# Layer 1's softmax sums over keys: from matmuls with ones to turned blocks on VectorE

## The chip, the core and the metric

The kernel runs on one core of a Trainium2 chip. The metric is the device time of one execution in microseconds (us). A core has five engines with their own instruction streams: TensorE (PE in the profile; its weight loads are PEld), VectorE (DVE), ScalarE (ACT), GpSimd (POOL) and SyncE (SP), which here issues nearly all DMA transfers. They meet through semaphores.

## What is computed

Two gated transformer-like blocks on x of 4 x 1024 x 512, in float32. The change is in the attention of the second block (layer 1):

```python
x = x + s * g                      # layer 0
xn = _layernorm(x, axis=-1)
# _L1_attn_ref(xn, wq, wk, wv, wo), 16 heads of 32
q, k, v = (proj(wq), proj(wk), proj(wv))
sin, cos = rope_tables(t, HD, dtype=x.dtype)
q, k = apply_rope(q, k, sin, cos)
att = jnp.einsum('bhqd,bhkd->bhqk', q, k) * (1.0 / math.sqrt(HD))
att = jax.nn.softmax(att, axis=-1)
y = jnp.einsum('bhqk,bhkd->bhqd', att, v)
y = y.transpose(0, 2, 1, 3).reshape(b, t, c)
return y @ wo.T
# then g = silu(_L1_ffn_ref(xn, ...)), and x + s * g is returned
```

The softmax needs, for every query and head, the maximum over 1024 keys, the exponentials, and their sum over keys, by which the weighted values are divided.

## The kernel before, in words

Layer 0 comes first, then layer 1's attention, then layer 1's feed-forward part. Only the attention concerns us. It works in 32 *units* (`units`, `nu` = 32): batch b (4), group g of four heads (4), half qh of the queries (512 each). Unit u has 8 key blocks kb of 128 keys (`TB` = 8). The loop over `s` goes through *slots*, eight per unit, and a slot holds work of several units at once:

- `top(u, j, pair, mx)`, two calls a slot, with u, j = divmod(s, 8): PE multiplies 128 queries with 512 keys for two heads into a tile `sq`, and VectorE takes the maximum over keys into `mx`. I call the two maxima of a slot a and b. At j = 7 the maxima of the unit are folded; `turn_max` one slot later transposes them on VectorE (`mt`) and sends them through DRAM (`turned_d`) into `mT`.
- `exps(e)` with e = s - 12 (`LAG` = 12): `expo` has PE multiply the keys of block kb with 512 queries of four heads into two tiles `sk`, adding the negative maxima by a matmul with `onesr` and `mT`; ScalarE takes the exponentials into `pT` (keys on partitions, 4 heads x 512 queries in the free axis; three buffers). Then the key blocks of a unit are added up into one tile `part`, by GpSimd (by VectorE in the last 12 slots). So unit u's key block 0 has its turn in slot 4 of unit u+1, and key block 7 in slot 3 of unit u+2.
- `weigh` one slot later: PE multiplies `pT` with the values into `y`. ScalarE copies `y` to `yr` after the last block.
- `total` and `divide` in slot 6 of unit u+2 (before the change): PE sums `part` over the 128 partitions, that is over keys, by a matmul with a tile of ones, four heads at once; the result `z` has the sum repeated over each head's 32 partitions. ScalarE copies it to `zs`, VectorE takes the reciprocal in four pieces, GpSimd multiplies `yr` with it into `yT`. Unit 30 (`nu - 2`) has no `part`: PE sums its eight `pT` directly. Unit 31 does so for its first four and adds up the others on VectorE.
- In between, `advance` puts quarters of other chains on PE: the projections of the next group of heads (`heads_in`: `wk`, `wq`, `v`), and the output projections `wo_out`, listed in `soon` for a later slot. For `wk` and `wq` each half is rotated: ScalarE copies it to `raw`, eight DMAs on SP put its halves into `rr`, VectorE multiplies (`wkT`, `wqT` with `cs`), and GpSimd does two operations (`rr` times `cs`, then the addition), called the `rr` pair here.

PSUM tiles of `sq` and `sk` come from one pool tag, `ring`, with three buffers in rotation, in the order sq a, sq b, sk, sk; projections use `acc1` with one buffer.

PE's order is that of the source (`manual_schedule` for PE). The instructions of the other engines are put in order by the framework's scheduler, by dependencies and its own estimate of when each can run; each engine then runs its instructions in the compiled order. `keep_in_program_order` pins single instructions.

Of the kernel before, what the change touches and what calls it, by code (L numbers as in the profile page):

```python
# [12 lines left out]
F32 = mybir.dt.float32  # L13
# [3 lines left out]
ALU = mybir.AluOpType  # L17
AX = mybir.AxisListType

P = 128  # L20
B, N, D = 4, 1024, 512
NT = B * N
H, HD = 16, 32
# [12 lines left out]
def kernel(ctx, tc, ins, out):  # L36
    nc = tc.nc
# [3 lines left out]
    dram = ctx.enter_context(tc.tile_pool(name="dram", bufs=1, space=bass.MemoryType.DRAM))  # L41
# [47 lines left out]
    def shared_tile(tag, name):  # L89
        return w0.tile([P, KD, D], F32, tag=tag, name=name)  # L90
# [155 lines left out]
    with ExitStack() as es:  # L246
# [4 lines left out]
        p2 = es.enter_context(tc.tile_pool(name="a0", bufs=2, reuse_waits="tile"))  # L251
# [318 lines left out]
    with ExitStack() as es:  # L570
# [3 lines left out]
        p2 = es.enter_context(tc.tile_pool(name="f0", bufs=2, reuse_waits="tile"))  # L574
# [126 lines left out]
        for g in range(NH0 * NBLK + 2 + 2 * TPB):  # L701
            blk, c = divmod(g, NH0)
            if g == NH0 * NBLK:

                for n in ("wk", "wq", "wv"):
# [3 lines left out]
                            out=W[n], in_=ins[n + "T"].rearrange("(k p) n -> p k n", p=P)  # L709
# [8 lines left out]
            for i in range(TPB):  # L718
                q = g - 2 - 2 * i
# [95 lines left out]
    with ExitStack() as es:  # L815
        wp = es.enter_context(tc.tile_pool(name="a1c", bufs=1, reuse_waits="tile"))
        p2 = es.enter_context(tc.tile_pool(name="a1", bufs=2, reuse_waits="tile"))

        def ring(name):
            return pp.tile([P, 2, 512], F32, tag="ring", name=name, bufs=3)  # L820

        def acc1(name):
            return pp.tile([P, 512], F32, tag="acc1", name=name)

        TB = N // P
# [4 lines left out]
        def load1(b):  # L830
# [15 lines left out]
        turned_d = [  # L846
            dram.tile([8, 512], F32, tag=f"turned{i}", name=f"turned_d{i}") for i in range(2)
        ]

        partner = []  # L850
        for i in range(2):
# [92 lines left out]
        def total(z, part, kb, n):  # L944

            for h in range(4):
                nc.tensor.matmul(  # L947
                    z[h * HD : (h + 1) * HD, :], lhsT=ones[:, :HD], rhs=part[:, h, :],
                    start=(kb == 0), stop=(kb == n - 1),
                )  # L950

        def divide(u, yr, z):

            b, g, qh = u
            zs = p2.tile([P, 512], F32, tag="zs", name=f"zs_{b}_{g}_{qh}", bufs=1)
            nc.scalar.copy(zs, z)
            yT = p2.tile([P, 512], F32, tag=f"yT{qh}", name=f"yT_{b}_{g}_{qh}", bufs=5 + qh)
            for c in range(TPB):
                cols = slice(c * P, (c + 1) * P)
                nc.vector.reciprocal(zs[:, cols], zs[:, cols])  # L960
            nc.gpsimd.tensor_tensor(yT, yr, zs, ALU.mult)
            yTs[b][g, qh] = yT
# [100 lines left out]
        def exps(e):  # L1063
            if not 0 <= e < TB * nu:
                return
            u, kb = divmod(e, TB)
            pT = pTs[e] = p2.tile([P, 4, 512], F32, tag="pT", name=f"pT_{e}", bufs=3)
            expo(u, kb, pT)


            if u == nu - 2:
                return
            k0 = TB // 2 if u == nu - 1 else 0
            add = nc.vector if e + LAG >= TB * nu else nc.gpsimd
            if kb == k0 + 1:
                parts[u] = p2.tile([P, 4, 512], F32, tag="part", name=f"part_{u}")
                add.tensor_tensor(parts[u], pTs[e - 1], pT, ALU.add)  # L1077
            elif kb > k0:
                add.tensor_tensor(parts[u], parts[u], pT, ALU.add)  # L1079
# [5 lines left out]
        units = [(b, g, qh) for b in range(B) for g in range(4) for qh in range(2)]  # L1085
        nu, LAG = len(units), TB + 4
        yTs = {b: {} for b in range(B)}
# [18 lines left out]
            tc.tile_pool(name="psuma", bufs=1, space=PSUM, reuse_waits="tile")  # L1106
        )
        must, spare = deque(), deque()
        mx, mTs, pTs, ys, parts, lates, soon = {}, {}, {}, {}, {}, {}, {}
        for s in range(TB * nu + LAG + 1):  # L1110

            e = s - LAG
            if s % (2 * TB) == 0 and s < TB * nu:

                assert not must
                n = s // (2 * TB) + 1
                if n < 4 * B:  # L1120
                    b, g = divmod(n, 4)

                    two = (nc.sync, nc.gpsimd) if s == 0 else (nc.sync, nc.sync)
                    must.extend(
                        heads_in(
                            b, g, acc1, {(w, h): two for w in ("wk", "wq") for h in range(2)}
                        )
                    )
                    if g == 3 and b + 1 < B:
                        load1(b + 1)  # L1130
                left = 2
            if s in soon and s < TB * nu:
                spare.extend(wo_out(*soon.pop(s), acc1))
            if s % 2 == 0:

                chain = None
                if spare and left and s < TB * nu:
                    chain = spare.popleft()
                    left -= 1
                elif must:  # L1140
                    chain = must.popleft()
            if s == 2 * TB:
                W["wo"] = shared_tile("wo", "wo")
                tc.keep_in_program_order(
                    nc.sync.dma_start(
                        out=W["wo"], in_=ins["woT"].rearrange("(k p) n -> p k n", p=P)
                    )
                )
            if s % 4 == 0 and s // 4 < TPB:
                lates[s + 2] = s // 4, late(s // 4)  # L1150
            if s < TB * nu:
                u, j = divmod(s, TB)
                if j == 0:
                    mx[u] = p2.tile([P, TPB, 4, 2], F32, tag="mx", name=f"mx_{u}")
                for pair in range(2):
                    top(u, j, pair, mx[u])
                if j == TB - 1:
                    m2 = twice[u % 2][:, :, :8].rearrange("p q (h c) -> p q h c", c=2)

                    w = p2.tile([P, TPB, 4, 2], F32, tag="m1", name=f"m1_{u}")  # L1160
                    nc.vector.tensor_reduce(
                        w[:, :, :, 0], mx.pop(u), AX.X, ALU.max, negate=True
                    )
                    for out, sign in ((w[:, :, :, 1], -1.0), (m2[:, :, :, 0], 1.0)):
                        nc.scalar.activation(
                            out.bitcast(F32R), w[:, :, :, 0], AF.Copy, scale=sign
                        )
                    nc.vector.tensor_reduce(m2[:, :, :, 1], w, AX.X, ALU.add)
            late_exp = s >= TB * nu
            if late_exp:  # L1170
                exps(e)
            if 1 <= e <= TB * nu:
                u, kb = divmod(e - 1, TB)
                if kb == 0:
                    ys[u] = pp.tile([P, 512], F32, tag="y", name=f"y_{u}")
                weigh(u, kb, pTs[e - 1], ys[u])
# [350 lines left out]
```

## Time and profile before

| | us |
|---|---|
| median of 3 runs (lowest, highest) | 3089.14 (3086.78, 3090.99) |
| the profiled execution | 3092.08 |
| its span, first to last instruction | 3090.2 |
| granted TensorE clock, mean | 0.996 |
| attention of layer 1: first `sq` maximum, first feed-forward matmul (`gate`) | 1163, 2598 |
| ScalarE busy in the span | 1173.7 |
| DMA issues on SP for `rr` in the span | 480 |

How to read it: a group line gives the kernel's line, the engine, the operation, what it writes and reads with shapes, the count, then busy time in us, the mean of one in ns, and the idle time of the engine just before them with what ended most of it. A timeline line gives start and length in us, engine, line, operation, tiles, shapes, how many instructions were merged into it, and in brackets the idle time before it and its releaser. A wait is put down to the engine that came last. The line of the chain of waits for `z` (L947) reads 1.2% of the span.

### The profile page before, as it was taken

The numbers are of one execution on the slowest core, as the hardware profiler recorded it, in microseconds if no ns is written. First come the engines' busy times: TensorE is split into PE (matmuls) and PEld (weight loads), VectorE is DVE, ScalarE is ACT, GpSimd is POOL, SyncE is SP. The second block draws the span as 40 slices with busy tenths as digits, with TensorE's granted clock in tenths as the row PEclk, the third lists the DMA queues.
The fourth block names the chain that finished last, engine by engine and source line by source line (L and its number), as shares of the span: only waits on it lengthen the run. The fifth ranks groups of instructions, "written<-read, shape, count | busy, mean of one in ns | idle before, by whom it ended". The sixth has DMA issues, their size and how long they took to land.

```text
span 3090.2 us, 61139 instructions
## 1 busy us (share of the span) xinstructions
PE 3038.3 (98%) x25985; PEld 1730.5 (56%) x25985; DVE 1788.3 (58%) x2569; ACT 1173.7 (38%) x1708; POOL 1557.9 (50%) x742
## 2 busy tenths in 40 slices
PE   9999999999999998999999999999999999999998
PEld 5555555578788873333334444333434436888886
DVE  4444555467777776555555555555555544566655
ACT  3111111145556542444444444444444454333332
POOL 1221212234443444888888988888988940001001
PEclk9999999999999999999999999999999999999999
DMA  4222232323223231100001000100000014222111
GB/s 137 86 86 86 86 86 72 127 96 100 95 92 110 96 129 52 36 9 9 9 18 42 16 10 15 43 16 14 10 18 15 13 46 152 82 69 75 58 52 56
DMA packets 113787, 186.81 MB, mean 60 GB/s; under 512 B 19809, under 2 KB 33633, under 8 KB 113377
## 3 DMA queue, kind: packets, MB, share of 16 engines
q1 hardware_dynamic: 106096, 161.30, 17.3%
q0 software_dynamic: 7280, 21.39, 1.9%
q8 instruction: 205, 3.36, 0.5%
q14 instruction: 78, 0.63, 0.1%
q10 hardware_dynamic: 128, 0.13, 0.0%
HBM read 115.11 MB, written 59.26 MB: 56 GB/s over the span
## 4 chain that ended last, share of the span: by engine, by line
PE 57%; DVE 1%; ACT 1%; POOL 1%; issue 0%; SPq 0%; DMA 0%; ACTq 0%; POOLq 0%; DVEq 0%
PE sk L1037 9%; PE sq L1007 8%; PE y L1056 8%; PE gate L1260 5%; PE up L1260 5%; PE dn L1282 5%; PE wo L862 4%; PE v1ps L862 3%; PE wk L862 3%; PE wq L862 3%; PE sk L1043 2%; PE z L947 1%; ACT pT L1048 1%; DVE zs L960 1%; POOL part L1079 0%; DVE mx L1011 0%
## 5 line engine op out<-in xcount | busy, mean ns | idle before, releaser
L1011 DVE TENSOR_REDUCE mx<-sq 128x2 f32<-128x1024 f32 x512 | 604.2, 1218 | 434.8 <-PE sq L1007 434.0
L1079 POOL TENSOR_TENSOR part<-part,pT 128x2048 f32<-128x2048 f32 x180 | 817.8, 4543 | 17.3 <-ACT pT L1048 8.9
L1048 ACT ACTIVATE pT<-sk 128x1024 f32<-128x1024 f32 x512 | 495.6, 1020 | 557.3 <-PE sk L1043 520.1
L1007 PE MATMUL sq<-wkT,wqT 32*128 32x512 f32 x2048 | 321.0, 639 | 10.0 <-ACT pT L1048 7.0
L1037 PE MATMUL sk<-wqT,wkT 32*128 32x512 f32 x2048 | 322.8, 641 | 0.8 <-DVE mx L1011 0.5
L1056 PE MATMUL y<-pT,v 128*32 128x512 f32 x2048 | 275.5, 608 | 0.1
L1304 POOL TENSOR_TENSOR th<-th,x 128x512 f32<-128x512 f32 x31 | 40.1, 1293 | 458.0 <-DVE th L1303 379.0
L646 PE MATMUL pj<-wpj,hp 128*128 128x512 f32 x1024 | 262.0, 396 | 4.0 <-DVE hp L606 4.0
L593 PE MATMUL fc<-xp,wfc 128*128 128x512 f32 x1024 | 259.0, 395 | 3.6 <-ACT h L598 2.8
L614 POOL TENSOR_TENSOR sums<-sums,h 128x512 f32<-128x512 f32 x112 | 163.1, 1456 | 195.0 <-ACT h L598 189.7
L1043 PE MATMUL sk<-mT,onesr 2*128 2x512 f32 x1024 | 235.7, 788 | 0.0
L382 PE MATMUL qk<-xnT,wqkv 128*128 128x512 f32 x512 | 228.7, 600 | 0.7 <-ACT xnT L156 0.7
L646 PEld LDWEIGHTS pj<-wpj,hp 128*128 128x128 f32 x1024 | 191.2, 188 | 51.9 <-DVE hp L606 10.5
L593 PEld LDWEIGHTS fc<-xp,wfc 128*128 128x128 f32 x1024 | 189.4, 188 | 47.2 <-ACT h L598 6.0
L606 DVE TENSOR_TENSOR hp<-h,hp 128x512 fp32r<-128x512 f32 x128 | 128.2, 1001 | 85.2 <-ACT hp L603 85.2
L1260 PE MATMUL gate<-xp,wf 128*128 128x512 f32 x704 | 174.2, 390 | 0.0
L1260 PE MATMUL up<-xp,wf 128*128 128x512 f32 x704 | 173.9, 389 | 0.0
L1037 PEld LDWEIGHTS sk<-wqT,wkT 32*128 32x128 f32 x2048 | 96.2, 184 | 138.3 <-issue 117.2
L1282 PE MATMUL dn<-wf,hp 128*128 128x512 f32 x704 | 173.6, 390 | 0.0
L1077 POOL TENSOR_TENSOR part<-pT,pT 128x2048 f32<-128x2048 f32 x30 | 136.4, 4548 | 72.1 <-ACT pT L1048 72.0
L1007 PEld LDWEIGHTS sq<-wkT,wqT 32*128 32x128 f32 x2048 | 89.9, 184 | 122.7 <-issue 85.5
L382 PEld LDWEIGHTS qk<-xnT,wqkv 128*128 128x128 f32 x512 | 95.0, 191 | 111.8 <-issue 104.5
(230 smaller groups left out, 4359.3 us busy)
## 6 DMA issues: line engine op xcount, KB each, us to landing
s<-s SPq DMA_DIRECT2D x96, 256.0 KB
xp<-xp_d SPq DMA_DIRECT2D x16, 1024.0 KB
x<-x SPq DMA_DIRECT2D x36, 256.0 KB
x<-in_x SPq DMA_DIRECT2D x32, 256.0 KB
raw_fc<-in_w_fcT SPq DMA_DIRECT2D x32, 256.0 KB
xp_d<-hi POOLq DMA_DIRECT2D x32, 256.0 KB, 2.7
xp_d<-xnT POOLq DMA_DIRECT2D x32, 256.0 KB, 2.9
x0r<-in_x SPq DMA_DIRECT2D x32, 256.0 KB
```

What stands on the lines that cost most here:

```text
L382: nc.tensor.matmul(a, lhsT=wqkv[k][:, c0 : c0 + P], rhs=xnTs[blk][:, k, :], start=(k == 0), stop=(k == KD - 1),)
L593: nc.tensor.matmul(a, lhsT=wfc[k][:, c * P : (c + 1) * P], rhs=xp[n][:, k, :].bitcast(F32R), start=(k == 0 and n == 0), stop=(k == KD - 1 ...
L646: nc.tensor.matmul(ds[i], lhsT=hparts[blk, c][n][:, i * P : (i + 1) * P], rhs=wpj[c], start=(c == 0 and n == 0), stop=(c == NH0 - 1 and n ...
L862: nc.tensor.matmul(out[r0 : r0 + HD, :], lhsT=lhsT[:, r0 : r0 + HD], rhs=rhs, start=start, stop=stop,)
L1007: nc.tensor.matmul(sq[:, hh, :], lhsT=qT[r, q0 : q0 + P], rhs=kT[r, n * 512 : (n + 1) * 512], start=True, stop=True,)
L1011: nc.vector.tensor_reduce(mx[:, qt, 2 * pair : 2 * pair + 2, n], sq, AX.X, ALU.max)
L1037: nc.tensor.matmul(sks[h // 2][:, h % 2, :], lhsT=kT[r, kb * P : (kb + 1) * P], rhs=qT[r, qh * 512 : (qh + 1) * 512], start=True, stop=False,)
L1048: nc.scalar.activation(pT[:, 2 * pair : 2 * pair + 2, :], sks[pair], AF.Exp, scale=QKS)
L1056: nc.tensor.matmul(y[r, :], lhsT=v[:, kb, r], rhs=pT[:, h, :], start=(kb == 0), stop=(kb == TB - 1),)
L1079: add.tensor_tensor(parts[u], parts[u], pT, ALU.add)
L1260: nc.tensor.matmul(a, lhsT=ws[n, c][:, k, :], rhs=xp[m][:, k, :], start=(k == 0 and m == 0), stop=(k == KD - 1 and m == 1),)
L1282: nc.tensor.matmul(ds[i], lhsT=hparts[blk, c][n][:, i * P : (i + 1) * P], rhs=w, start=(c == 0 and n == 0), stop=(c == NH1 - 1 and n == 1),)
```

## The change

The matmuls `total` for units 0 to 30 go. In their place VectorE transposes the `part` tile in blocks of 32 x 32 (`sums_of`, eight chunks of 256 columns) and sums each turned block along its rows; `gather` turns the collected 64 columns back and sends them through DRAM (`groups_d`) so that the four groups of 32 partitions lie beside one another; `invert` adds the four, takes the reciprocal of 64 columns on 32 partitions, and sends it through DRAM (`inverse_d`), from where four DMAs spread a row each over 32 partitions into `zs`; `times` multiplies on GpSimd. Unit 30 now has a `part` too: GpSimd adds its blocks up to 3, VectorE the blocks 4 to 7. In the source a unit's sums stand in slots 6 to 11 counted from the start of unit u+2, `gather` in slot 12, `invert` in slot 14, `times` in slot 16. The output projections start two slots after `times`, and in the last 16 slots up to 8 of them may start. `divide` stays for unit 31.

```diff
+        def sums_of(u, part, c):
+            if c == 0:
+                groups[u] = p2.tile([P, 64], F32, tag="groups", name=f"groups_{u}", bufs=1)
+            t = p2.tile([P, 256], F32, tag="keys", name=f"keys_{u}_{c}", bufs=1)
+            nc.vector.transpose(t, part.rearrange("p h q -> p (h q)")[:, c * 256 : (c + 1) * 256])
+            nc.vector.tensor_reduce(
+                groups[u][:, 8 * c : 8 * c + 8], t.rearrange("p (c a) -> p c a", a=HD), AX.X, ALU.add
+            )
+
+        def gather(u):
+            back = p2.tile([P, 64], F32, tag="back", name=f"back_{u}", bufs=1)
+            nc.vector.transpose(back, groups.pop(u))
+            at = groups_d[u % 2]
+            nc.sync.dma_start(out=at, in_=back)
+            sides[u] = p2.tile([P, 256], F32, tag="keys", name=f"sides_{u}", bufs=1)
+            nc.sync.dma_start(
+                out=sides[u][:HD, :].rearrange("c (i x) -> c i x", i=4),
+                in_=at.rearrange("(i c) x -> c i x", i=4),
+            )
+
+        def invert(u):
+            b, g, qh = units[u]
+            inv = p2.tile([P, 64], F32, tag="inv", name=f"inv_{u}", bufs=1)
+            nc.vector.tensor_reduce(
+                inv[:HD, :], sides.pop(u)[:HD, :].rearrange("c (i x) -> c x i", i=4), AX.X, ALU.add
+            )
+            nc.vector.reciprocal(inv[:HD, :], inv[:HD, :])
+            at = inverse_d[u % 2]
+            nc.sync.dma_start(
+                out=at.rearrange("a c b -> c a b"),
+                in_=inv[:HD, :].rearrange("c (a b) -> c a b", a=2),
+            )
+            zss[u] = p2.tile([P, 512], F32, tag="zs", name=f"zs_{b}_{g}_{qh}", bufs=1)
+            for h in range(4):
+                row = at[h // 2, 16 * (h % 2) : 16 * (h % 2) + 16, :]
+                nc.sync.dma_start(
+                    out=zss[u][h * HD : (h + 1) * HD, :],
+                    in_=row.rearrange("c b -> (c b)").partition_broadcast(HD),
+                )
+
+        def times(u, yr):
+            b, g, qh = units[u]
+            yT = p2.tile([P, 512], F32, tag=f"yT{qh}", name=f"yT_{b}_{g}_{qh}", bufs=5 + qh)
+            nc.gpsimd.tensor_tensor(yT, yr, zss.pop(u), ALU.mult)
+            yTs[b][g, qh] = yT
...
@@ exps
-            if u == nu - 2:
-                return
...
@@ the loop over s
-                left = 2
+                left = 2 if n < 4 * B else TB
...
+            zu, at = divmod(s - 6, TB)
+            zu -= 2
+            for u, i in ((zu - 1, at + TB), (zu, at)):
+                if u == nu - 2:
+                    if i == 0:
+                        for c in range(8):
+                            sums_of(u, parts[u], c)
+                        parts.pop(u)
+                    elif i == 1:
+                        gather(u)
+                    elif i == 3:
+                        invert(u)
+                    elif i == 5:
+                        times(u, ys.pop(u))
+                        soon[s] = units[u][0], units[u][2], yTs[B - 1]
+                elif 0 <= u < nu - 2:
+                    if i < 6:
+                        for c in ((0, 1), (2,), (3,), (4, 5), (6,), (7,))[i]:
+                            sums_of(u, parts[u], c)
+                        if i == 5:
+                            parts.pop(u)
+                    elif i == 6:
+                        gather(u)
+                    elif i == 8:
+                        invert(u)
+                    elif i == 10:
+                        times(u, ys.pop(u))
+                        b, g, qh = units[u]
+                        if g == 3:
+                            soon[s + 2] = b, qh, yTs[b]
...
-                if u >= nu - 2:
+                if u == nu - 1 and kb < TB // 2:
                     if kb == 0:
                         z_last = acc1(f"z_{u}")
-                    if u < nu - 1 or kb < TB // 2:
-                        total(z_last, pTs[e - 1], kb, TB)
+                    total(z_last, pTs[e - 1], kb, TB)
...
-                    yr = p2.tile([P, 512], F32, tag="yr", name=f"yr_{u}", bufs=1)
+                    yr = p2.tile([P, 512], F32, tag="yr", name=f"yr_{u}")
...
-                    if u == nu - 2:
-                        divide(units[u], ys.pop(u), z_last)
-                        soon[s] = units[u][0], units[u][2], yTs[B - 1]
             held = 0
-            zu = (s - 6) // TB - 2
             if s % TB == 0 and 0 < s <= TB * nu:
                 turn_max(s // TB - 1)
-            if s % TB == 6 and 0 <= zu < nu - 2:
-                z = ring(f"z_{zu}")[:, 0, :] if zu == nu - 3 else acc1(f"z_{zu}")
-                total(z, parts.pop(zu), 0, 1)
-                divide(units[zu], ys.pop(zu), z)
-                b, g, qh = units[zu]
-                if g == 3:
-                    soon[s + 4] = b, qh, yTs[b]
-            elif s in lates:
+            if s in lates:
                 late_turn(*lates.pop(s))
```

More of the change, by code (lines that the diff above doesn't have):

```diff
@@ L848 @@
         ]
+        groups_d = [dram.tile([P, 64], F32, tag=f"groups{i}", name=f"groups_d{i}") for i in range(2)]
+        inverse_d = [
+            dram.tile([2, HD, HD], F32, tag=f"inverse{i}", name=f"inverse_d{i}") for i in range(2)
+        ]
         partner = []
@@ L952, in divide @@
+        def times(u, yr):
[3 more added lines that the diff above has]
+            yTs[b][g, qh] = yT
         def divide(u, yr, z):
             b, g, qh = u
-            zs = p2.tile([P, 512], F32, tag="zs", name=f"zs_{b}_{g}_{qh}", bufs=1)
+            zs = p2.tile([P, 512], F32, tag="mT", name=f"zs_{b}_{g}_{qh}")
             nc.scalar.copy(zs, z)
@@ L1108 @@
         must, spare = deque(), deque()
+        groups, sides, zss = {}, {}, {}
         mx, mTs, pTs, ys, parts, lates, soon = {}, {}, {}, {}, {}, {}, {}
```

## The prediction

> **What bounds the kernel now.** First the page's busy times, then the window of layer 1's attention (about 1163 to 2598 us), then one unit of it instruction by instruction.
>
> ```profile
> PE 3038.3 (98%) x25985; PEld 1730.5 (56%) x25985; DVE 1788.3 (58%) x2569; ACT 1173.7 (38%) x1708; POOL 1557.9 (50%) x742
> ...
> L1011 DVE TENSOR_REDUCE mx<-sq 128x2 f32<-128x1024 f32 x512 | 604.2, 1218 | 434.8 <-PE sq L1007 434.0
> L1079 POOL TENSOR_TENSOR part<-part,pT 128x2048 f32<-128x2048 f32 x180 | 817.8, 4543 | 17.3 <-ACT pT L1048 8.9
> ```
>
> PE is busy all the time. VectorE waits only for PE's next `sq`, and GpSimd, 4.54 us per key block, is the engine with least to spare in this stage: 1115 of the 1300 us between 1200 and 2500 (its row of the busy times there). A slot with a quarter of a projection in it takes 5.25 us (the `sq` starts 1246.15, 1251.39 in the timeline), one without 4.6 us. Now unit 2's slot 4, the place the change touches:
>
> ```profile
> 1251.33 9.15 POOL L1079 TENSOR_TENSOR part<-part,pT 128x2048 f32<-128x2048 f32 x2
> 1251.39 1.14 PE L1007 MATMUL sq<-wkT,wqT 32*128 32x512 f32 x8
> ...
> 1253.17 2.34 DVE L1011 TENSOR_REDUCE mx<-sq 128x2 f32<-128x1024 f32 x2
> ...
> 1257.16 1.14 PE L1007 MATMUL sq<-wkT,wqT 32*128 32x512 f32 x8
> ...
> 1264.40 1.07 PE L947 MATMUL z<-part,ones 128*32 128x512 f32 x8
> ...
> 1266.44 3.38 DVE L960 RECIPROCAL zs<-zs 128x128 f32<-128x128 f32 x4
> ```
>
> Unit 0's partial sums are complete when GpSimd ends at 1251.33 + 9.15 = 1260.48; I call this moment T. VectorE has by then done both maxima of slot 4 (1253.17) and is on to slot 5. PE uses the sums in slot 6 (1264.40), so nobody waits. (Units of odd number end later, with GpSimd's backlog: unit 1 at 1306.6, some 12 us behind the start of its slot 4.)
>
> **The change, part by part.**
>
> *Removed.* A group of `z` matmuls costs 1.04 to 1.07 us; 30 groups on `part` and 8 on unit 30's `pT` go: 38 x 1.04 = 39.5 us of PE. Four reciprocals (3.38 us) per unit go from VectorE and a `zs` copy (0.59) from ScalarE. The `wo` chains start eight slots later: 0 us, since the same 32 chains only trade places with empty slots of PE that the trace has at 4.6 us each.
>
> *Where the new work stands.* The source emits the eight transposes and sums of a unit over slots 6 to 11, one or two a slot, which would fit VectorE's idle 2.8 us. But only PE's order is written by hand; the others are ordered by the scheduler. The compiled order of the changed kernel, which can be listed without running it, has on VectorE for unit u (u from 2 to 31, sums of unit u-2; a and b are the two maxima of a slot):
>
> ```
> 4a, pair 0, 4b, pairs 1 to 7, back, 5a, 5b, inv sum, reciprocal, 6a, 6b ...
> ```
>
> For u = 3, 5, 7, 9 only the transpose of pair 0 stands before 4a and `back` behind 5a (for 31 behind 5b). So pair 0, which needs the finished `part` (T), is queued ahead of maximum 4b, and all pairs stand ahead of 5a. VectorE stands still from the end of 4a to T. Behind it waits 4b; for 4b waits PE's first `sq` of slot 5 (`ring` has three buffers: `sq` a of slot 5 takes that of `sq` b of slot 4, the second `sk` of a slot that of its `sq` a). That VectorE keeps its order is seen in the trace:
>
> ```profile
> 1308.57 3.39 DVE L960 RECIPROCAL zs<-zs 128x128 f32<-128x128 f32 x4 [1.33 <-ACT zs L956]
> ...
> 1311.88 2.29 DVE L1011 TENSOR_REDUCE mx<-sq 128x2 f32<-128x1024 f32 x2
> ...
> 1314.65 1.92 ACT L1048 ACTIVATE pT<-sk 128x1024 f32<-128x1024 f32 x2
> ...
> 1314.95 0.31 DVE L1016 STREAM_TRANSPOSE mt<-m 128x128 f32<-128x128 f32 x1
> ```
>
> VectorE idled 1.33 us before the reciprocals, and the maxima ran behind them. [...] If the queue could pass a waiting instruction, the sum would be that of rival C below.
>
> *Prices not in the trace.* A transpose of 128x256: the row of 128x128 is 0.31 us, so between 0.31 and 0.62; I take the middle, 0.47. The sum 128x256 to 8: between the rows of 32 elements (0.186) and of 1024 (1.218), on the line between them 0.42. A pair is 0.88 (0.73 to 1.04), eight 7.1 us. [...] `back` (64 columns) 0.25; reciprocal of 64 columns about half of the 0.9 us row, 0.48. A transfer that the next one waits for:
>
> ```profile
> 1315.29 2.79 SPq L1023 DMA_DIRECT2D turned_d<-mt  x4
> 1319.33 1.16 SPq L1026 DMA_DIRECT2D mT<-turned_d  x4
> ```
>
> The last of four begins at 1317.4, the reader at 1319.33: 1.9 us a hop (landing of `rr` is 1.7/1.9/3.9 at least, median, most; I keep 1.9 and 2.9). Issues cost 0.3 (`mT`) to 0.7 us (`turned_d`) each. The seven new issues of a unit stand on SP ahead of `rr`, `turned_d` and `mT` and hold it some 9 us; `rr` pays (below), `mT` not: issued about 29 us behind T, needed in slot 4 at 44.
>
> *One unit after T, in us from T.* Pair 0 to 0.9, 4b to 2.1 (PE starts slot 5 here), pairs 1 to 7 to 8.3, `back` 8.55, 5a 9.8, 5b 11.0. Only at 9.8 can PE do the second `sk` of slot 5. From such a maximum's end to both exponentials' end took 3.5 us in the lines after the reciprocals above, where PE waited for it too (first maximum 1313.05, exponentials 1316.57). So GpSimd gets key block 1 of the next unit at 13.3 and adds until 17.85. PE's slot 6 starts at 9.8 + 1.4 (`sk`) + 1.5 (rest of the projection) = 12.7. The transfers: `groups` out 8.6 to 10.5, `sides` in to 12.45, sum 12.9, reciprocal 13.4, `inverse` out 15.35, four `zs` in, landed 18.1 to 19.3, say 18.7. GpSimd's product `yT`, which in its compiled order stands right behind the first add, ends at 20.0.
>
> *Then the next T.* In units of odd number from 11 GpSimd's order is: first add, `yT`, `rr` pair, two adds, pair, two adds, pair, two adds. The first `rr` load stands on SP behind the four `zs` (about 17.2) and takes what it took before:
>
> ```profile
> 1349.39 5.30 SPq L916 DMA_DIRECT2D rr<-raw_wq  x8
> ...
> 1356.19 1.27 POOL L920 TENSOR_TENSOR rr<-rr,cs 128x512 f32<-128x512 f32 x1 [2.69 <-DMA rr<-raw_wq]
> ```
>
> 5.3 us and 1.5 more to landing: 24.0. Three pairs (2.55 each) and six adds (4.55) from there: 24.0 + 7.65 + 27.3 = 59.0. Units 9, 17 and 25 have their first pair before, but the second load lands only at about 36, which gives the same end. Units 1 to 7 have two pairs: 56.4; unit 29 none, 20.0 + 27.3 = 47.3. (Before, loads hidden behind GpSimd's backlog; now the backlog is gone and every load is waited for.) In units of even number GpSimd has no or one pair and would be done at 47.3 to 49.9; PE reaches slot 3 at 12.7 + 5 x 5.25 = 38.95, its exponentials end 5.95 later, the add 4.55 later: 49.5. I take 49.7. Intervals between the 30 T's: 4 x 56.4 + 10 x 59.0 + 47.3 + 14 x 49.7 = 1558.7 us. Before, the first T was 1260.48, and the last, from GpSimd's row that starts at 2489.07 and runs 27.54, was 2516.61: 1256.1 us. Difference **+302.6 us**. The 39.5 us of PE are not subtracted: in these intervals GpSimd and VectorE's wait set the end.
>
> *The tail.* Before, `wo` of the last pair starts 52 us after the last T (2568.7). After: GpSimd's three adds of unit 30 end at 29.1 (behind `yT`), VectorE's four (2.29 each) at 38.3, its eight pairs at 45.3, the four hops, sum, reciprocal and product at 57: **+5 us**; unit 30's `z` groups were hidden in that length.
>
> Sum: 302.6 + 5 = +308. On the profiled execution (3092.08, its span 3090.2) 3400; it lies 3 us over the median, so 3089.1 + 308 = **3397 us**.
>
> **Bounds.** Pairs of 0.73 or 1.04 us: 8 x 0.15 x 30 = 36 us each way. `zs` issues: 0.6 x 15 = 9 us.
>
> **Rivals.**
>
> A (above), 0.66: 3340 to 3460, by these bounds and about as much again for the hops.
>
> B, 0.16: GpSimd's waits vanish (`yT`'s and the `rr` loads land in time), and only its work counts: 13.3 + 7 x 4.55 + 1.3 + two or three pairs = 51.6 or 54.1. 4 x 51.6 + 10 x 54.1 + 47.3 + 14 x 49.5 = 1488, so +232, with the tail 3326. For it: the waits that I put in are only 0.9 and 4.0 us. Against: SP issues `rr` in order behind the four `zs`, and GpSimd waited 2.7 us for such loads already.
>
> C, 0.06, faster (0.01 of it within 0.2%): the sums run where the source puts them (slots 6 to 11), covered by VectorE's idle 2.8 us a slot (1.76 us for two pairs). Then PE keeps the 39.5 us, and the tail's transfers hide behind `sk` and `y`: 3050. It holds if T lies before the end of maximum 4a. Against it: T was 6 us behind that end for unit 0, and the last add alone takes 4.55 us behind exponentials that end within slot 4.
>
> D, 0.12: hops of 2.9 us: `yT` 4 us later, the `rr` loads 5, maximum 6a 2: about 8 us a pair of units, 14.5 x 8 = 116: 3513.
>
> The likeliest is A: 3397. The range, 3290 to 3490, holds A and B and ends before D. 0.2% is 6 us, about what a measurement of this kernel tells from no change: faster 0.05, same 0.01, slower 0.94.
>
> **What would show it.** VectorE idle before its first L965 of a unit, released by `part`, some 5 to 15 us; maximum 4b behind it; PE idle on `sq` released by VectorE once a unit; GpSimd's idle on `part` first adds about 13 us a unit and on `rr` and `yT` some us; T's 50 and 59 us apart in turn. Wrong if the L965 rows lie spread over six slots with PE as busy as before, or if the maxima pass them.

## The result and the profile after

| us | before | after |
|---|---|---|
| median of 5 runs (lowest, highest) | 3090.99 (3086.78, 3092.61) | 3491.54 (3490.99, 3497.28) |
| span of the profiled execution | 3090.2 | 3495.5 |
| granted TensorE clock, mean | 0.996 | 0.932 |
| first T, last T | 1260.5, 2516.6 | 1260.75, 2912.57 |

The changed kernel takes 1.130 times as long (95% interval 1.128 to 1.132). The sign and most of the size were forecast; the time lies 94 us above the forecast. Line numbers shift: the maxima are L1066 now, the additions L1130 and L1132, the turned blocks L965. The page, busy times, clock row and groups:

```profile
PE 3187.4 (91%) x25681; PEld 1777.4 (51%) x25681; DVE 1943.9 (56%) x3038; ACT 1158.8 (33%) x1677; POOL 1571.3 (45%) x745
...
PEclk9999999999999997879798989899888988999999
...
L1132 POOL TENSOR_TENSOR part<-part,pT 128x2048 f32<-128x2048 f32 x182 | 825.7, 4537 | 77.2 <-ACT pT L1103 72.9
L1066 DVE TENSOR_REDUCE mx<-sq 128x2 f32<-128x1024 f32 x512 | 605.1, 1215 | 437.0 <-PE sq L1062 436.9
...
L1062 PE MATMUL sq<-wkT,wqT 32*128 32x512 f32 x2048 | 364.5, 712 | 156.3 <-DVE mx L1066 150.4
...
L1130 POOL TENSOR_TENSOR part<-pT,pT 128x2048 f32<-128x2048 f32 x31 | 140.3, 4525 | 404.1 <-ACT pT L1103 404.1
...
L965 DVE STREAM_TRANSPOSE keys<-part 128x256 f32<-128x256 f32 x248 | 110.1, 444 | 229.1 <-POOL part L1132 222.6
```

The same rows of the page before:

```profile
PEclk9999999999999999999999999999999999999999
...
L1007 PE MATMUL sq<-wkT,wqT 32*128 32x512 f32 x2048 | 321.0, 639 | 10.0 <-ACT pT L1048 7.0
...
L1077 POOL TENSOR_TENSOR part<-pT,pT 128x2048 f32<-128x2048 f32 x30 | 136.4, 4548 | 72.1 <-ACT pT L1048 72.0
```

Two things are to be seen. A ring of waits that was not there before: GpSimd stands 13 us a unit ahead of its first addition (404.1 over 31; before 72.1 over 30), VectorE 7.4 us a unit ahead of the turned blocks, PE 150 us ahead of `sq` (before 10). And PE's busy time is 149 us *more* than before, though 304 of its instructions are gone: the mean `sq` matmul takes 712 ns (before 639), and the clock row, all nines before, has sevens and eights in just this stage. The view of waits for 1200 to 2950 us (sum in us, how often, longest):

```profile
POOL part L1130 <- ACT pT L1103: 404.1, 31, 18.1
DVE keys L965 <- POOL part L1132: 222.6, 30, 14.2
...
PE sq L1062 <- DVE mx L1066: 150.4, 26, 9.4
...
PE sk L1092 <- DVE mx L1066: 110.0, 31, 10.9
```

One unit of the timeline from its T, 1902.40, with the clock of the same stretch in a view by windows behind it. Such a line gives a stretch and its length, then the busy us of PE, its weight loads, VectorE, ScalarE and GpSimd (instructions in brackets), and last the granted clock, the DMA share and GB/s:

```profile
1902.40 0.45 DVE L965 STREAM_TRANSPOSE keys<-part 128x256 f32<-128x256 f32 x1 [9.59 <-POOL part L1132]
...
1904.48 2.09 PE L1062 MATMUL sq<-wkT,wqT 32*128 32x512 f32 x8 [8.80 <-DVE mx L1066]
...
1911.04 2.32 DVE L1066 TENSOR_REDUCE mx<-sq 128x2 f32<-128x1024 f32 x2
...
1912.28 1.22 PE L1092 MATMUL sk<-wqT,wkT 32*128 32x512 f32 x2 [2.37 <-DVE mx L1066]
...
1914.71 2.79 PE L866 MATMUL v1ps<-wv,xnT 128*32 128x128 f32 x48
...
1916.50 4.52 POOL L1130 TENSOR_TENSOR part<-pT,pT 128x2048 f32<-128x2048 f32 x1 [11.57 <-ACT pT L1103]
```

```profile
1905.00:1908.00 3.00, 3.00 (x16) 0.40 (x12) 2.79 (x7) 0.00 (x0) 0.00 (x0) 0.50 0.03 5
1908.00:1911.00 3.00, 1.91 (x24) 0.67 (x16) 2.76 (x8) 0.00 (x0) 0.00 (x0) 0.96 0.00 0
...
1914.00:1917.00 3.00, 3.00 (x48) 2.13 (x48) 1.12 (x2) 1.94 (x2) 0.50 (x1) 0.50 0.02 3
...
1920.00:1923.00 3.00, 3.00 (x80) 2.01 (x72) 1.48 (x2) 1.10 (x2) 2.26 (x2) 1.00 0.02 5
```

The second `sk` of slot 5 starts 9.88 us after T; the forecast had 9.8. Then it parts from the forecast: the clock is at half, so the rest of slot 5 takes 5.1 us instead of 2.9. Slot 6 starts at T + 15.0 (forecast 12.7), and the next T comes at 52.4 instead of 49.7.

### The profile page after: what moved, and what is told of

Same layout as the page of the kernel before. It is cut to its first block, busy times and chain, and to the rows that moved or that the text cites. A ratio compares the mean times of both kernels' runs of the same rounds, so it can differ in the third digit from the quotient of the medians.

```text
span 3495.5 us, 61321 instructions
## 1 busy us (share of the span) xinstructions
PE 3187.4 (91%) x25681; PEld 1777.4 (51%) x25681; DVE 1943.9 (56%) x3038; ACT 1158.8 (33%) x1677; POOL 1571.3 (45%) x745
## 4 chain that ended last, share of the span: by engine, by line
PE 39%; POOL 9%; DVE 8%; SPq 3%; issue 2%; DMA 2%; ACT 1%; POOLq 0%; ACTq 0%; DVEq 0%
POOL part L1132 8%; PE sk L1092 6%; PE sq L1062 5%; PE gate L1335 5%; PE up L1335 5%; PE dn L1357 4%; PE y L1111 4%; DVE keys L965 3%; PE wo L866 3%; DVE mx L1066 3%; DVE groups L966 3%; SPq L920 2%; PE v1ps L866 2%; PE wk L866 2%; PE sk L1098 1%
## 5 line engine op out<-in xcount | busy, mean ns | idle before, releaser
L1132 POOL TENSOR_TENSOR part<-part,pT 128x2048 f32<-128x2048 f32 x182 | 825.7, 4537 | 77.2 <-ACT pT L1103 72.9
L1066 DVE TENSOR_REDUCE mx<-sq 128x2 f32<-128x1024 f32 x512 | 605.1, 1215 | 437.0 <-PE sq L1062 436.9
L1062 PE MATMUL sq<-wkT,wqT 32*128 32x512 f32 x2048 | 364.5, 712 | 156.3 <-DVE mx L1066 150.4
L1092 PE MATMUL sk<-wqT,wkT 32*128 32x512 f32 x2048 | 401.0, 692 | 110.1 <-DVE mx L1066 110.0
L1130 POOL TENSOR_TENSOR part<-pT,pT 128x2048 f32<-128x2048 f32 x31 | 140.3, 4525 | 404.1 <-ACT pT L1103 404.1
L1111 PE MATMUL y<-pT,v 128*32 128x512 f32 x2048 | 300.7, 660 | 0.1
L1098 PE MATMUL sk<-mT,onesr 2*128 2x512 f32 x1024 | 284.4, 842 | 0.0
L1092 PEld LDWEIGHTS sk<-wqT,wkT 32*128 32x128 f32 x2048 | 115.8, 197 | 278.5 <-DVE mx L1066 154.4
L1062 PEld LDWEIGHTS sq<-wkT,wqT 32*128 32x128 f32 x2048 | 101.7, 206 | 282.3 <-DVE mx L1066 161.7
L965 DVE STREAM_TRANSPOSE keys<-part 128x256 f32<-128x256 f32 x248 | 110.1, 444 | 229.1 <-POOL part L1132 222.6
L593 PEld LDWEIGHTS fc<-xp,wfc 128*128 128x128 f32 x1024 | 189.4, 188 | 47.3 <-ACT h L598 6.1
```

The lines of the kernel that those rows point to most:

```text
L593: nc.tensor.matmul(a, lhsT=wfc[k][:, c * P : (c + 1) * P], rhs=xp[n][:, k, :].bitcast(F32R), start=(k == 0 and n == 0), stop=(k == KD - 1 ...
L1062: nc.tensor.matmul(sq[:, hh, :], lhsT=qT[r, q0 : q0 + P], rhs=kT[r, n * 512 : (n + 1) * 512], start=True, stop=True,)
L1066: nc.vector.tensor_reduce(mx[:, qt, 2 * pair : 2 * pair + 2, n], sq, AX.X, ALU.max)
L1092: nc.tensor.matmul(sks[h // 2][:, h % 2, :], lhsT=kT[r, kb * P : (kb + 1) * P], rhs=qT[r, qh * 512 : (qh + 1) * 512], start=True, stop=False,)
L1098: nc.tensor.matmul(sks[h // 2][:, h % 2, :], lhsT=onesr[r, :], rhs=mTs[u][r, :].bitcast(F32R), start=False, stop=True,)
L1111: nc.tensor.matmul(y[r, :], lhsT=v[:, kb, r], rhs=pT[:, h, :], start=(kb == 0), stop=(kb == TB - 1),)
```

## The experiments

Theories: **W**, the forecast's (the burst of sums waits for `part` ahead of maxima, and the ring of waits closes), with **K** added after the result: a wait of several us also costs PE its clock. Rivals: the sums cost by themselves, the transfers do, or the low clock is only a sign. A kernel called "pinned" has VectorE's L965 transposes, `back` and the sum in `invert` in `keep_in_program_order`; all numbers of changed intervals are between the starts of pair 0 of consecutive units.

**1. The order of the source.** The changed kernel, pinned:

```diff
-            nc.vector.transpose(t, part.rearrange("p h q -> p (h q)")[:, c * 256 : (c + 1) * 256])
+            tc.keep_in_program_order(
+                nc.vector.transpose(t, part.rearrange("p h q -> p (h q)")[:, c * 256 : (c + 1) * 256])
+            )
...
-            nc.vector.transpose(back, groups.pop(u))
+            tc.keep_in_program_order(nc.vector.transpose(back, groups.pop(u)))
```

> The changed kernel with one thing different: on VectorE the transposes of the eight pairs, the transpose back and the sum before the reciprocal are pinned where the source has them (slots 6 to 11, 12 and 14). Theory (the compiled order costs the time: wait for the part, burst, and what follows): VectorE's idle time covers the pairs, PE keeps the z groups, about 3050 us, 40 below before. Rival (the new work itself costs the time: the pairs, seven transfers a unit, GpSimd's product waiting for them): stays above 3300 us.

Measured 3074.17 us (four runs, 3067.82 to 3077.51), 0.993 of the kernel before (0.991 to 0.996), clock 0.993. The two kernels lie 417 us apart, and what was edited is the place of the sums on VectorE; experiment 2 shows that pinning by itself is not what helps. In the source's places the same sums, transfers and products are a small gain, about half of what rival C had; experiment 9 looks at its size.

**2. The same order, written out.** A control: the eight pairs and `back` are emitted inside the loop of the maxima (pair 0 between 4a and 4b, the others behind 4b), pinned.

> Control: the same pins, but the sums are written into the source where the changed kernel's compiled order has them (pair 0 between the maxima of slot 4, pairs 1 to 7 and the transpose back behind them, sum and reciprocal behind slot 5's). Theory: as the changed kernel, 3490 us within 20. If pinning itself, or the order on the other engines, mattered, it would lie away from that.

Measured 3483.29, clock 0.936: the order makes the time, and pinning as such does not help. It differs from the changed kernel in four units, 3, 5, 7 and 9, where the compiled order has pair 0's transpose ahead of 4a; its intervals sum to 10 us less.

**3. The burst without the wait for `part`.** Pinned, all eight pairs in one slot where `part` is long complete:

```diff
-                    if i < 6:
-                        for c in ((0, 1), (2,), (3,), (4, 5), (6,), (7,))[i]:
-                            sums_of(u, parts[u], c)
-                        if i == 5:
-                            parts.pop(u)
+                    if i == 2:
+                        for c in range(8):
+                            sums_of(u, parts[u], c)
+                        parts.pop(u)
```

> As the source-order kernel, but all eight pairs of a unit in one slot, slot 8, where the part is long complete: the burst without the wait. Theory: 7 us of pairs against some 2.8 us of idle time and 1.5 us that a maximum may be late: PE stands 3 us a unit, 90 us in all, 3140 us; PE's clock stays full. Rival (the burst is what costs the 400 us): above 3300 us.

**4. The wait without the burst.** Pinned, pair 0 between 4a and 4b, the others in the source's slots.

> As the source-order kernel, but pair 0 stands between the two maxima of slot 4, ahead of the finished part: the wait without the burst. Theory: GpSimd gets key block 1 some 8 us after T instead of 13; T's 49 and 44 us apart in turn, 92 us more than before, 3180 us; if PE's clock falls in the waits as it does in the changed kernel, up to 50 us more. Rival (the wait is hidden, the burst costs): below 3100 us.

Measured 3253.92 and 3299.49. Either part alone costs far more than was worked out for it (3140, and 3180 with up to 50 more if the clock falls), and together, +180 and +225 over the pinned kernel, they make up nearly the whole +417. The timeline of the burst shows a part that was missing:

```profile
1816.64 0.70 PE L1096 MATMUL sk<-wqT,wkT 32*128 32x512 f32 x2 [3.19 <-DVE mx L1070]
...
1818.55 2.79 PE L866 MATMUL wo<-wo,yT 128*32 128x256 f32 x24
1821.27 2.09 PE L1066 MATMUL sq<-wkT,wqT 32*128 32x512 f32 x8
```

PE waits 3.19 us, and then the same matmuls that take 1.50 and 1.14 us elsewhere take 2.79 and 2.09, for about 7 us. Over the window 1266 to 2660 the mean clock is 0.94, that is some 164 us at half speed, worth, by an estimate that halves them, at most 82 of the 114 us by which the forecast of the burst missed. In the other kernel GpSimd's `part` is waited for as in the changed one:

```profile
DVE keys L966 <- POOL part L1136: 181.3, 25, 11.3
PE sq L1066 <- DVE mx L1070: 156.0, 25, 10.1
```

**5. A smaller dose.** The burst as six pairs in one slot and two in the next (`if i in (2, 3)` with `range(6)` and `(6, 7)`).

> The pinned order with six pairs of transpose and sum in one slot and two in the next (the burst had all eight in one slot: 3254 us, a wait of 3.2 us on TensorE each time, and about 8 us at a lower clock behind it). Two pairs less are 1.74 us less, so TensorE should wait about 1.5 us per unit. If such a short wait leaves the clock at full: 3074 + 30 x 1.5 = about 3119 us, and the mean clock as in the pinned kernel. Rival, any wait of more than a microsecond lowers the clock: 2.5 to 3 us more per unit, 3190 to 3210 us.

Measured 3161.05, between the two. PE's wait is 1.4 us as worked out, and the clock part came out half: in this unit the wait leaves the clock alone, in the next it does not (timeline, then a window of each).

```profile
1824.93 0.70 PE L1096 MATMUL sk<-wqT,wkT 32*128 32x512 f32 x2 [1.39 <-DVE mx L1070]
...
1870.22 0.70 PE L1096 MATMUL sk<-wqT,wkT 32*128 32x512 f32 x2 [1.33 <-DVE mx L1070]
...
1871.50 2.58 PE L866 MATMUL wo<-wo,yT 128*32 128x256 f32 x24
```

```profile
1827.00:1830.00 3.00, 3.00 (x40) 0.88 (x32) 2.08 (x4) 1.60 (x3) 3.00 (x2) 1.00 0.02 3
...
1872.00:1874.00 2.00, 2.00 (x20) 0.64 (x12) 0.97 (x3) 1.41 (x2) 0.45 (x1) 0.50 0.00 0
```

By windows of 15 us from 1270 to 2530 the clock falls in 12 of some 28 units, ten times for 3.3 us and twice for 7 (0.89 over 15 us is 3.3 us at half). At half price, again an estimate, that is some 24 of the 87 us over the pinned kernel. The rest, 2.1 us a unit, is the stall, which was sized too low at 1.5: in a unit whose clock holds, that slot takes 7.73 us instead of 5.25 (starts of `sq` 1819.92 and 1827.65).

**6. Filled slots.** The written-out order; where PE has no projection or output chain, a chain of 128-row matmuls that nobody reads runs:

```diff
                 elif must:
                     chain = must.popleft()
+                elif 2 * TB <= s < TB * nu:
+                    chain = idle(s)
```

> The order of the changed kernel, written out, with one addition: where TensorE's slots have no projection or output chain (the last four of every 16 slots of batch 0, some at the end), a chain of 128-row matmuls like a quarter projection runs, whose result nobody uses. Nothing is left out, work is added. If the light 32-row work of these slots is what keeps the granted clock at half after the wait, the four intervals between units of batch 0 that end in such slots fall from 60, 56, 57 and 62 us to the 52.4 us of the later ones, though TensorE has more to do: 3483 - 26 = about 3457 us, and the mean granted clock rises. Rival, the long slots have another cause (a wait, a transfer): the time stays at 3483 or grows by the added matmuls, up to 3495.

Measured 3502.67, clock 0.941: a miss, longer by 19 us. The four intervals of batch 0 stay at 57.3, 56.6, 57.8 and 56.3 us, though their mean clock is 0.85 to 0.89 where the written-out kernel had 0.79 to 0.86. (The 60, 56, 57 and 62 us of the expectation are the changed kernel's; the written-out one has 56.3, 58.8, 56.3 and 54.8. Of the 19 us, 14 stand behind the last T.) What ends them is GpSimd, as in this line of the filled kernel (the changed kernel has the same wait, 2.74 us, at 1718.71):

```profile
1709.17 1.26 POOL L924 TENSOR_TENSOR rr<-rr,cs 128x512 f32<-128x512 f32 x1 [2.73 <-DMA rr<-raw_wk]
```

Six short intervals, those into units 4, 6, 8, 10, 18 and 26, have an `rr` pair in the middle of GpSimd's additions whose load is not there yet. So the claim that only light work keeps the clock low there isn't shown, and these intervals were not the place to test the clock.

**7. PE kept busy while it waits.** The written-out order, with products of zeros added to `y`:

```diff
+        def nothing(n, pT, y):
+            for _ in range(n):
+                for h in range(4):
+                    nc.tensor.matmul(
+                        y[h * HD : (h + 1) * HD, :], lhsT=zero, rhs=pT[:, h, :],
+                        start=False, stop=False,
+                    )
```

> The order of the changed kernel, written out (3483 us), with TensorE kept at work while it waits for VectorE: matmuls with a tile of zeros, added to y, so that the result stays. In units of odd number nine rounds of about 1 us stand before the wait of 9 us at the end of slot 4, in some of even number four before a wait of 5.6, and three rounds in slot 5 before the second wait (1.6 to 4.2 us). The last block of y moves behind them. VectorE's order and GpSimd's work are the same, work is added. If the clock that falls behind a wait costs time by itself: TensorE's slot 6 then starts 2.7 us earlier, the eight short intervals of 52.4 us fall to about 49.7, GpSimd gets its second key block 0.8 us earlier in the long ones, and with a little in batch 0 that is 35 to 50 us less, about 3440 us, mean clock over 0.97. Rival, the clock is a sign of the waits and costs nothing by itself: 3483 us or more.

Measured 3496.82, clock 0.976: a miss again, with a confounder. Moving the last block of `y` let the scheduler put GpSimd's product ahead of its first addition. The view of waits:

```profile
POOL yT L1008 <- DMA zs<-inverse_d: 423.3, 24, 19.8
```

Two short intervals at full clock (by windows 1.00) took 49.5 us, but two others at full clock, from 1900.4 and 2692.0, took 51.6 and 54.0: there GpSimd's product waited 15.5 and 17.9 us ahead of the addition. The expectation of the next experiment names only the first two. This run decides nothing.

**8. The same with GpSimd's order held.** The first addition and the product are pinned as the written-out kernel has them:

```diff
-            nc.gpsimd.tensor_tensor(yT, yr, zss.pop(u), ALU.mult)
+            tc.keep_in_program_order(nc.gpsimd.tensor_tensor(yT, yr, zss.pop(u), ALU.mult))
...
+                if s % TB == TB // 2 + 1 and 2 * TB <= s < TB * nu:
+                    times(s // TB - 2, ys.pop(s // TB - 2))
```

> As the kernel that keeps TensorE busy with zeros, but with GpSimd's first addition and its product yT pinned in the order of the changed kernel. In the run before the scheduler had put the product ahead of the addition, where it waited 17 to 20 us for zs in 24 units, so that ScalarE and TensorE waited for a pT buffer and the clock fell there; only two short intervals kept the full clock from end to end, and they took 49.5 us. If that order was what spoilt it: the eight short intervals of 52.4 us of the written-out kernel become 49.5, the long ones of 60.3 become about 59.4, batch 0 a little shorter: 8 x 2.9 + 10 x 0.9 + some 5 = 37 us less than 3483, about 3446 us, clock over 0.98. Rival, the lower clock is not what costs: 3480 us or more, and the short intervals stay at 52 to 55 us.

Measured 3447.02, clock 0.984: 36 us less than the written-out order, with *more* work on PE. The timeline at the place of the wait, then windows that are a long and two short intervals of this kernel:

```profile
1767.04 7.91 PE L1175 MATMUL y<-pT,zero 128*32 128x512 f32 x72
...
1776.20 1.14 PE L1066 MATMUL sq<-wkT,wqT 32*128 32x512 f32 x8 [0.40 <-DVE mx L1070]
...
1784.00 0.70 PE L1098 MATMUL sk<-wqT,wkT 32*128 32x512 f32 x2 [1.45 <-DVE mx L1070]
...
1785.29 1.52 PE L866 MATMUL v1ps<-wv,xnT 128*32 128x128 f32 x48
```

```profile
2217.28:2266.72 49.44, 47.54 (x612) 19.25 (x608) 27.64 (x38) 17.90 (x23) 35.55 (x10) 1.00 0.18 62
2266.72:2325.42 58.70, 55.10 (x608) 20.26 (x604) 30.04 (x43) 18.52 (x24) 40.57 (x15) 1.00 0.08 17
2325.42:2376.48 51.06, 48.67 (x608) 20.16 (x604) 27.62 (x38) 18.01 (x23) 35.56 (x10) 0.97 0.06 19
```

At full clock a short interval takes 49.44 to 49.52 us, six times out of six; at a mean of 0.97, which is some 3 us at half clock, 51.06, twice; in the written-out kernel, at a mean of 0.88, 52.46 (the last line; six of its eight lie between 52.4 and 52.6, and the two at 0.89 take 51.0):

```profile
1889.73:1942.19 52.46, 48.01 (x576) 19.92 (x576) 27.60 (x38) 17.49 (x23) 35.50 (x10) 0.88 0.06 19
```

The place where it acts can be read off: in both kernels the second `sk` of slot 5 starts 9.88 us after T (here at 1784.00, T being 1774.12), but slot 6 starts at T + 12.6 here and at T + 15.0 in the written-out and in the changed kernel. In the long intervals the clock acts through GpSimd's second `rr` load: in the one from 2266.72, at full clock, it is there in time (58.7 us), in the one from 1823.56, at 0.97, GpSimd waits 1.48 us for it (60.2). The lower clock is thus a cause of its own in these kernels (a short interval takes 49.44 us at 1.00 and 52.46 at 0.88): it falls with the wait and lengthens what comes behind it.

**9. What the removed matmuls were worth.** The kernel before without the 30 `z` groups on `part`, their `zs` and reciprocals, so that these units are not divided (GpSimd copies `yr` in place of the product):

> The kernel before with the 30 groups of z matmuls on part, their copies to ScalarE's zs and their reciprocals left out: those units are not divided by their sums. It shows what the removed matmuls are worth at most. If each of the 30 groups is worth its 1.04 us: 31 us less than before, in the loop up to the last maximum (before: 2530.1 us). Rival, they are worth only what the pinned kernel got there, 21 us, since something else in the loop has a part in its pace.

Measured 3078.0 beside 3089.9. The last maximum ends at 2514.6 instead of 2530.1: 15.5 us, 0.52 a group and not 1.04. The pinned kernel's last maximum ends at 2509.1, 5.5 us earlier still, and it gives 4 back in the tail. So this run isn't the upper bound that it was meant to be. The timelines of slot 6, where `z` stood, show why. Its mean length over units 2 to 30 is 6.10 us before, 5.80 here and 5.36 in the pinned kernel; the other seven slots together take 37.4, 37.3 and 37.5. In this run the loop still keeps the first piece of the projection (8 or 16 matmuls) out of the place between `y` and `sk` in slot 6, as it did for `z`, so `sk` follows `y` at once:

```profile
1515.69 1.06 PE L1056 MATMUL y<-pT,v 128*32 128x512 f32 x8
1516.69 1.76 PE L1037 MATMUL sk<-wqT,wkT 32*128 32x512 f32 x6
...
1519.03 1.93 PE L862 MATMUL wq<-xnT,wq 128*32 128x256 f32 x32
```

Both `sk` of slot 6 together take 2.0 us in the mean there, against 1.4 before, behind `z`, and 1.6 in the pinned kernel, behind that piece of the projection. In part a `z` group had thus covered a stretch in which `sk` is held up (by what, was not traced); where its place is filled by other work, slot 6 is 0.74 us shorter, which over 29 units is most of the pinned kernel's gain.

**10 and 11. The tail of the pinned kernel.** From the last maximum's end to the first feed-forward matmul it takes 71.9 us (before: 67.7; the expectations count from the start of the last two maxima, 2.3 us earlier), with PE waiting 4.61 us for `pT`. In one variant unit 30 is handled as before the change; in the other its `invert` stands behind unit 31's first addition.

> The pinned order, with the last unit but one as before the change (its sums over keys by matmuls on pT, nothing added up). The pinned kernel's tail, from the last maximum to the first feed-forward matmul, is 74.2 us against 70.0 before, with a wait of 4.6 us of TensorE for pT. If that wait comes from unit 30's sums on VectorE, the tail returns to about 70: 3074 - 4 = 3070 us. Rival, the eight groups of matmuls that come back cost their 8 us on top: about 3078 us.

> The pinned order, with the sum and reciprocal of the last unit but one moved behind VectorE's first addition for the last unit. In the pinned kernel VectorE stands there for 3.2 us until a transfer lands, with that addition queued behind it, and ScalarE and TensorE wait 5.0 and 4.6 us for it. If this order is what costs: 3074 - 4.6 = about 3069 us. Rival, the same wait appears elsewhere in the tail: 3074.

Unit 30 by matmul: a tail of 69.2 us, most of the way as forecast, and 3079.38 us, 0.995 of before (0.994 to 0.997). `invert` later: a tail of 71.5, 3080.72 us, 0.995 (0.994 to 0.997); the wait on `pT` shrinks to 0.23 us, and a new one takes its place, by the timeline:

```profile
2555.50 1.08 PE L866 MATMUL wo<-wo,yT 128*32 128x256 f32 x8 [4.72 <-POOL yT L1008]
```

So the rival holds there: the chain of unit 30's sums, four transfers and the product sets the end. The intervals of these two and of the pinned kernel overlap; which of the three is best isn't settled. All three beat the kernel before by about half a per cent.

## Why the prediction was wrong by 94 us, by its own steps

The intervals between the T's, as the forecast groups them; the last column is the kernel of experiment 8, in which PE mostly keeps its clock (a mean of 0.88 to 1.00 in these intervals):

| us | forecast | after | clock mostly kept |
|---|---|---|---|
| 15 long ones | 862.9 | 885.6 | 871.1 |
| 8 short ones | 397.6 | 417.7 | 398.9 |
| 6 short ones with a late `rr` pair | 298.2 | 348.6 | 331.6 |
| sum | 1558.7 | 1651.8 | 1601.6 |

Over the 1256.1 before, the forecast had +302.6 and the trace shows +395.7. Of the 93 us between, 50 are the distance to the last column. They stand for the clock, with a reservation: that kernel is built on the written-out order, whose 29 intervals sum to 1641.9, so that 40 us are measured at one order and 10 are the four units of batch 0 whose order differs. Another 33 lie in the six intervals with a late `rr` pair, which still have some clock in them (the four of batch 0 at 0.88 to 0.94), the rest 8 in the long intervals and 1 in the short (the second `rr` load is late as well, by 1.7 us in the interval from 1842.19). The tail, below, adds 4.

**The step that failed** is the sentence "PE's slot 6 starts at 9.8 + 1.4 (`sk`) + 1.5 (rest of the projection) = 12.7", with "PE reaches slot 3 at 12.7 + 5 x 5.25" behind it: PE's work after the wait was priced by rows of a kernel in which PE hardly waits. Slot 6 starts at T + 15.0 in most units, because the rest of slot 5 runs at half clock, and at T + 12.6 in experiment 8, where the clock stays up: what the forecast put at nothing is the clock. In four stretches of batch 0, whose order differs, slot 6 starts at T + 11.9, but it and the slots behind it are long: from 1680.06 slots 6 and 7 take 8.2 and 7.6 us, where a slot without a projection takes 4.6. The windows of that stretch of the changed kernel, from 1669.81 on, behind a wait of 9.38 us:

```profile
1671.00:1680.00 9.00, 9.00 (x34) 2.56 (x30) 8.56 (x18) 1.94 (x2) 0.00 (x0) 0.50 0.02 4
1680.00:1689.00 9.00, 9.00 (x36) 2.80 (x34) 3.33 (x5) 2.39 (x3) 5.30 (x2) 0.50 0.13 34
1689.00:1698.00 9.00, 9.00 (x34) 2.75 (x32) 3.38 (x6) 3.71 (x6) 4.99 (x2) 0.50 0.02 5
...
1704.00:1707.00 3.00, 3.00 (x44) 1.19 (x44) 0.43 (x1) 1.94 (x2) 0.80 (x1) 1.00 0.00 0
```

The trace of before hardly shows it: from 1230 us to the last maximum no wait of PE is over 0.75 us, and the clock is at half once there, for 3.4 us from 1402.6. What a wait of 5 to 9 us on PE once a unit does to the clock was thus not shown there; the forecast put such a wait in and took full speed behind it, without a word on the clock. The runs here agree on the fall behind such long waits (in the changed kernel behind 30 of 30 of 3.75 us and over); they show it behind some shorter ones too, and agree less on the return, as the last section says.

**The second failed step**: "In units of even number GpSimd has no or one pair and would be done at 47.3 to 49.9". Work was counted and the wait for the load left out, although the forecast wrote for the odd units that "every load is waited for". Measured in the written-out kernel, T at 1662.68: first addition from 13.8, seven additions 31.9, `yT` and its waits 2.0, waits for `pT` 1.7, the load 2.7, the pair 2.6: 54.8.

**Right**: the mechanism and its place. VectorE is idle ahead of L965 30 times, released by `part`; maximum 4b is queued behind it; GpSimd's idle is 13.0 us a unit as forecast; at full clock the intervals are 49.4 and 58.7 against 49.7 and 59.0. The tail is +9 instead of +5: GpSimd's third addition of unit 30 ends at T + 33.1, not 29.1, with waits of 2.3 us for `zs` and 2.7 for `pT`. **Prices**: transpose 0.444 (0.47 taken), its sum 0.42 (0.42), `back` 0.24 (0.25), reciprocal 0.54 (0.48), the sum of `invert` 0.58 (0.42). From the issue of `groups_d` to that of its reader 1.5 us passed (1.9). **Rivals**: C was wrong for the changed kernel and right of the pinned one in kind; its 3050 took the matmuls at their full 1.04 us. D's 3513 is the nearest of the four numbers to 3491.5, but by luck: its condition, hops of 2.9 us, did not hold (medians of 1.5 and 1.4 from the issue of a writer to that of its reader). B fails, since GpSimd's waits for `rr` are there (66 us in the stage).

## What to carry to other kernels

When a wait is put on an engine whose clock falls behind such waits, as PE's did here behind each of the changed kernel's 30 waits of 3.75 us and over, price the work behind the wait too: the row of a kernel that never waits is no price for one that does. Order on the engines that a scheduler fills is part of the change: read the compiled order, and pin the one or two engines where a waiting instruction stands ahead of work others need. And when a wait is removed from a chain in an experiment, look whether the scheduler moved something else, as it did in experiment 7, or left a hole where the removed work stood, as in experiment 9.

## What the runs showed of the hardware

No length of wait separates the cases. In the written-out kernel one unit holds two:

```profile
1831.53 1.14 PE L1066 MATMUL sq<-wkT,wqT 32*128 32x512 f32 x8 [2.17 <-DVE mx L1070]
...
1839.33 1.22 PE L1096 MATMUL sk<-wqT,wkT 32*128 32x512 f32 x2 [4.17 <-DVE mx L1070]
```

Behind 2.17 us the `sq` runs at full speed (clock 1.00 from 1831 to 1834), behind 4.17 the clock is at half for about 5 us more (0.50 from 1840 to 1843, 0.74 from 1843 to 1846). In the attention stage of the changed kernel each of the 30 waits of PE of 3.75 us and over came with a spell at half clock, of 6.83 to 40.96 us; of the waits of 1.3 to 1.4 us in experiment 5, 12 did and 12 didn't. A wait isn't even needed: in the kernel before, the spell from 1402.6 follows slots without a projection, with no wait over 0.4 us near it. In the clock records of the kernel before and of the changed kernel, save at the end of the execution, every spell at half clock lasts 3.41 us or a multiple of it (before, 3.41 each time; in the changed kernel up to 40.96); in experiment 5's loop ten last some 3.3 us by the windows and two some 7.

The return was the greater surprise: about 7 us for experiment 3's spell above, but in the changed kernel still 34 us behind the wait, from 1669.8 to 1703.5, at a clock of 0.50 with PE busy 33.69 of the 33.70 us. Up to `wk` at 1700.90 it ran only 32-row `sq` and `sk`, the `mT` matmuls and `y` there, and the clock came back 2.6 us after `wk`, with 128 rows, began; but in the written-out kernel it came back within 16 us of 1664.8 (0.50 up to 1680, 0.88 from 1680 to 1683), before any `wk` (the next at 1689.14), on the same work. What decides the length is open.
